# Layer 0 of a two-layer attention kernel: products in 128x32 column tiles, scores in 32x64 tiles

## The chip, the cores and the metric

One core of one Trainium2 chip. The metric is the device time of one execution in microseconds (us), median of three runs.

## The reference, cut to what matters

The input is one block of 128 rows, 256 tokens in a row, 256 channels at a token, in float32. Two layers follow one another; each normalizes over groups of channels, attends within each row, and adds its result to its input.

Layer 0, for every one of the 128 rows (R = 256 tokens, 8 heads of 32 channels):

```
xn = group_norm(x)
gate = sigmoid(xn @ gate_proj); q, k, v = split(xn @ qkv_proj)
sim = softmax(q k^T / sqrt(32)) + bias          # bias: from pair_repr, the same for all rows
out = ((sim v) * gate) @ out_proj
x = x + out
```

Layer 1 does the same without gate and bias, with 4 heads of 64 channels, biases on its projections, and a band: a token sees only tokens up to 16 places away.

## The kernel before, in words

TensorE does all the products; everything is float32. A matrix product in the code becomes two MATMUL and two LDWEIGHTS instructions in the trace (line 784 is passed 2048 times, and the profile has 4096), so every count below is twice that of the code.

In layer 0 a step of the loop over `s` (line 913) takes one row. The engines' order of work is written out by hand: the loop is inside `tc.manual_schedule` (line 903), and each of TensorE, ScalarE and VectorE takes its instructions in the order of the calls. GpSimd and the DMA queue of SyncE are ordered by the framework. TensorE's order in a step is:

1. `scores(s, 0)` (line 777): q and k of four heads. The four heads lie on four strips of 32 partitions, so each product has 32 contraction rows and 128 output columns: a 32x128 tile, and the four heads j use four row strips side by side and write four PSUM banks `sims[j]`. Line 784 does it for two halves `kt` of the keys. ScalarE takes the exponentials from PSUM (line 797).
2. `sum_heads(s - 1)` (line 822): the softmax sums `zs` (line 830) and the product of the bias with v, `bv` (line 816, through `products`), for the row before. These have 128 contraction rows and 32 output columns (one head): 128x32 tiles, four side by side for j = 0 to 3.
3. `attend(s - 1)` (line 853): the product of the exponentials with v, `av`, also through line 816 in 128x32 tiles. VectorE then scales and gates (lines 861, 862, 864) and writes `at`, the input of the output projection.
4. `scores(s, 1)`: the other four heads, again 32x128.
5. `stretch` (line 885): the projections of a coming pair of rows, q and k in even steps, v and gate in odd ones, by `two_of_them` (line 616) with two `Seven` objects. A `Seven` makes a product of two rows by two blocks of channels from seven 128x128 products instead of eight (`product`, line 585). For q, k and the gate (line 594) the weights are the stationary operand and 256 tokens stream; for v (line 598, `by_token`) 128 tokens are the stationary operand and 128 weight columns stream. Between the sevens' last products, `next(po, None)` puts in the output projection of the row before (`one_by_one`, line 702; the product is line 708).

All of step 5 uses the whole array, 128 contraction rows by 128 output columns.

Banks of PSUM: `psum(banks0, "0", 5, 0)` (line 346) gives five banks that score tiles and projections take in rotation, and one each for `zs`, `bv` and `av`. Layer 1 uses the class `Summed`, which inherits `product` from `Seven`, and `one_by_one` for its last rows. Its own products for v (line 1045), scores (1066), attention (1107) and sums (1119) are in tiles of 128x64, 64x64 and 64x32.

Of the kernel before, what the change touches and what calls it, by code (L numbers as in the profile page):

```python
# [15 lines left out]
P = 128  # L16
# [4 lines left out]
H0, D0 = 8, 32  # L21
H1, D1 = 4, 64
BAND = 16
A, B = 4, 32
KB = 64
# [14 lines left out]
def conv_preact_kernel(  # L40
# [14 lines left out]
    nc = tc.nc  # L55
# [20 lines left out]
    def proj_bank(name):  # L76
        return bank("proj", name)

    def sim_bank(name):
        return bank("sim", name)  # L80
# [27 lines left out]
    out_sb = const.tile([P, 2, C], F32, name="out_sb")  # L108
# [29 lines left out]
    for base, per_row, per_group in ((0, 1, -CG), (CG - 1, -1, CG)):  # L138
        nc.gpsimd.affine_select(
            out=within.rearrange("p (g c) -> p g c", c=CG), in_=within.rearrange("p (g c) -> p g c", c=CG),  # L140
# [4 lines left out]
    w_out_t = const.tile([P, 2, C], F32, name="w_out_t")  # L145
# [8 lines left out]
    class Quarters:  # L154


        def __init__(self, pool, source, col, name):
            self.source, self.col = source, col
            self.sums = pool.tile([P, len(NS), P], F32, name=f"sums_{name}")
# [406 lines left out]
    def row_sums(t, x, engine):  # L566
# [3 lines left out]
        engine.tensor_tensor(t[:, 2], x[:, 3], x[:, 2], ALU.subtract)  # L570
        engine.tensor_tensor(t[:, 3], x[:, 1], t[:, 1], ALU.subtract)

    class Seven:


        def __init__(self, pool, weights, x, t, name, tag, by_token=False):
            self.weights, self.x, self.t, self.by_token, self.name = weights, x, t, by_token, name
# [7 lines left out]
        def product(self, n, two=None, first=False):  # L585
            x, t = self.x, self.t
            moving = {1: x[:, 0], 2: x[:, 1], 3: x[:, 3], 4: t[:, 3], 5: t[:, 0], 6: t[:, 1], 7: t[:, 2]}[n]
            out = two if n == 2 else self.ps[:, 1 if n in (3, 5) else 0, :]

            first = first or n == 1  # L590
            flags = dict(stop=n in (2, 3, 4), skip_group_check=True)
            weights = self.weights.stationary(n)
            if not self.by_token:
                nc.tensor.matmul(out, lhsT=weights, rhs=moving, start=first, **flags)  # L594
                return
            for t2 in range(2):
                cols = slice(t2 * P, (t2 + 1) * P)
                nc.tensor.matmul(out[:, cols], lhsT=moving[:, cols], rhs=weights, start=first and t2 == 0, **flags)  # L598

        def take(self, what):  # L600
            if what == "15":
# [44 lines left out]
            p.add_mid()  # L646

    class Summed(Seven):

# [47 lines left out]
            if n in (1, 5):  # L699
                amid(n)  # L700

    def one_by_one(w, at, name, done):

        ps = proj_bank(name)
        done(ps)
        for m in range(2):
            for kt in range(2):
                nc.tensor.matmul(  # L708
                    ps[:, m, :], lhsT=w[:, kt, m * P : (m + 1) * P], rhs=at[:, kt, :],
                    start=(kt == 0), stop=(kt == 1),  # L710
                )
                yield
# [10 lines left out]
    with ExitStack() as both:  # L723
# [20 lines left out]
        with ExitStack() as lay0:  # L744
            row = lay0.enter_context(tc.tile_pool(name="row0", bufs=2))
            att = lay0.enter_context(tc.tile_pool(name="att0", bufs=2))
            st, hd, outs = {}, {}, {}
# [29 lines left out]
            def scores(s, half):  # L777
                i, r = divmod(s, 2)
                q, k = res["q", i], res["k", i]
                sims = [sim_bank(f"sim{s}_{half}_{j}") for j in range(4)]  # L780
                for kt in range(2):
                    for j in range(4):
                        p0 = D0 * j
                        nc.tensor.matmul(  # L784
                            sims[j][:, kt, :],
                            lhsT=k[p0 : p0 + D0, 2 * r + half, kt * P : (kt + 1) * P],
                            rhs=q[p0 : p0 + D0, 2 * r + half, :],
                            start=True, stop=True,
                        )
                ex = att.tile([P, 4, 2, R], F32, tag="ex", name=f"ex{s}_{half}", bufs=4)  # L790
                both = att.tile([P, 4, R], F32, tag="both", name=f"both{s}_{half}")
                hd[s, half] = (ex, both)


                def weigh(js):
                    for j in js:
                        nc.scalar.activation(ex[:, j], sims[j], AF.Exp, scale=1.0 / math.sqrt(D0))  # L797

                weigh(range(3))
                return lambda: weigh((3,))  # L800
# [84 lines left out]
            def stretch(names, i, s, rest=lambda: None):  # L885

                po = iter(())
                if s >= 0:
                    po = one_by_one(out_sb, st[s]["at"], f"po{s}", lambda ps: st[s].update(po=ps))
                if 2 * i >= S:  # L890
                    rest()
                    for _ in po:
                        pass
                    return
                f, g = (
                    Seven(row, quarters[w], xns[i], tss[i], f"{w}{i}", w, by_token=(w == "v")) for w in names
                )
                for w, p in zip(names, (f, g)):
                    res[w, i] = p.to
                two_of_them(row, f, g, f"{names}{i}", po, rest)  # L900


            with tc.manual_schedule(engines={mybir.EngineType.PE, mybir.EngineType.Activation, mybir.EngineType.DVE}):
                for s in range(2):
                    normal(s)
                sum_rows(0)
                stretch("qk", 0, -1)
                for s in range(2, 4):
                    normal(s)
                stretch("vg", 0, -1)  # L910
                sum_rows(1)
                most1 = Most(st1, stats1, 3, 1)
                for s in range(S):
                    scores(s, 0)()
                    zs = sum_heads(s - 1)
                    join_tiles(s, 0, 0)
                    divide(s - 1, zs)
                    if s % 2 == 0:
                        e = res["g", s // 2]
                        nc.scalar.activation(e, e, AF.Exp, scale=-1.0)  # L920
                    z = hd[s - 1, "z"][0] if s > 0 else None
                    rest = ((0, 2), (1, 0), (1, 2))
                    if s < S - 1:
                        attend(s - 1)
                        last_exp = scores(s, 1)
                        if s == 4:
                            for weights in quarters1.values():
                                weights.sum()
                        stretch(("qk", "vg")[s % 2], s // 2 + 1, s - 1, last_exp)
                        for half, j in rest:  # L930
                            join_tiles(s, half, j)
                        least(s - 1, z)
                        if s >= S - 3:
                            most1.join(s - S + 3)
                        normal(s + 4)
                        if s % 2 == 1:
                            sum_rows((s + 3) // 2)
                        finish(s - 1)
                    else:

                        scores(s, 1)()
                        for half, j in rest:
                            join_tiles(s, half, j)
                        least(s - 1, z)
                        attend(s - 1)
                load1(0)
                load1(1)
                warm = proj_bank("warm")

                def keep_on(n):  # L950

                    for _ in range(n):
                        nc.tensor.matmul(warm[:, 0, :], lhsT=ident, rhs=out_sb[:, 0, :], start=True, stop=True)

                divide(S - 1, sum_heads(S - 1))
                last_z = hd[S - 1, "z"][0]
                attend(S - 1)
                for s in (S - 2, S - 1):
                    if s == S - 1:
                        keep_on(4)  # L960
                    for _ in one_by_one(out_sb, st[s]["at"], f"po{s}", lambda ps: st[s].update(po=ps)):
                        pass
                    finish(s)
                mean1, rstd1 = channel_columns(st1, most1, 1, keep_on)
                least(S - 1, last_z)
# [5 lines left out]
        with ExitStack() as lay:  # L971
# [3 lines left out]
            st, hd, outs = {s: {} for s in range(S)}, {}, {}  # L975

            weights = [att.tile([P, 2, 2 * WROW], F32, name=f"1p{i}", bufs=1) for i in range(4)]
# [36 lines left out]
            def project(s):  # L1014

                if s < 0:
                    return iter(())
                return one_by_one(w_out_t, st[s]["at"], f"1po{s}", lambda ps: st[s].update(po=ps))

            ats, ats_t, outputs, last_ots = {}, {}, {}, {}  # L1020

# [221 lines left out]
            with tc.manual_schedule(engines={  # L1243
# [12 lines left out]
                for i in range(last):  # L1256
                    s = 2 * i
# [84 lines left out]
    with tc.If(sure < P):  # L1342
        with ExitStack() as lay:
# [4 lines left out]
            for t in range(2):  # L1348
# [4 lines left out]
                out=bv_row.rearrange("p a b -> p (a b)"), in_=b_in[2 * C : 3 * C].partition_broadcast(P)  # L1353
# [130 lines left out]
            for g in range(S // XG):  # L1484
                x3 = two.tile([P, XG, 2, R], F32, tag="x3", name=f"x3_{g}")
                nc.sync.dma_start(out=x3, in_=rows(x1, g * XG, XG))
                for k in range(0, XG, 2):
                    for half in range(2):
                        nc.vector.bn_stats(
                            out=stats2[:, half, (g * XG + k) // 2, :], in_=x3[:, k : k + 2, half, :]  # L1490
# [32 lines left out]
```

## Time and profile before

| what | value |
|---|---|
| median of three runs | 3169.02 us (3168.06 to 3169.51) |
| profiled execution, span from first to last instruction | 3173.6 us |
| before the first scores of layer 0 | 206 us |
| layer 0, the loop over rows | 206 to about 2079 us |
| layer 1 | about 2089 us to the end |
| mean granted TensorE clock | 0.991 of full speed |

The profile gives one execution. PE is TensorE's matmuls, PEld its weight loads, which overlap with them, DVE is VectorE, ACT ScalarE, POOL GpSimd. A tile is written contraction rows by output columns, 32*128 for instance, and a shape behind it is that of the moving operand. The end of a matmul is modelled, so times below are taken between starts.

### The profile page before, as it was taken

What the parts mean: (1) busy time and instruction counts of PE and PEld (TensorE: products, weight loads), DVE (VectorE), ACT (ScalarE), POOL (GpSimd) and SP (SyncE); (2) the same over time, 40 slices, a digit from 0 to 9 for tenths busy, and PEclk for the clock granted to TensorE, in tenths of its full rate; (3) what the DMA queues carried; (4) which work ended last, traced back from release to release, by engine and by line L of the source; (5) the groups of instructions that cost most, each with busy time, mean ns of one, the idle gap of its engine ahead of it and who ended that gap; (6) DMA issues with size and microseconds to landing.
All of it is one profiled execution on the core that took longest, in us unless ns stands there. A gap on an engine that the chain in (4) does not pass through costs nothing.

```text
span 3173.6 us, 87645 instructions
## 1 busy us (share of the span) xinstructions
PE 3097.4 (98%) x36859; PEld 2384.0 (75%) x36859; DVE 2558.2 (81%) x4140; ACT 1870.3 (59%) x4064; POOL 1613.4 (51%) x1651
## 2 busy tenths in 40 slices
PE   7889999999999999999999999999999999999997
PEld 5567777777777777777777777768888888888886
DVE  4669999999999999999999999956666666666665
ACT  4656666666666666666666666645555555555553
POOL 3034444444444444444444444347777777777774
PEclk8989999999999999999999999999999999999999
DMA  9931111111111111111111111004444444444343
GB/s 379 424 109 42 41 41 34 41 35 39 37 35 41 35 39 37 38 38 35 41 34 37 39 37 39 28 28 102 96 101 101 93 99 102 100 97 101 91 100 69
DMA packets 357105, 242.44 MB, mean 76 GB/s; under 512 B 276072, under 2 KB 342112, under 8 KB 350560
## 3 DMA queue, kind: packets, MB, share of 16 engines
q1 hardware_dynamic: 355808, 234.39, 27.1%
q8 instruction: 292, 4.78, 0.6%
q0 software_dynamic: 752, 2.36, 0.2%
q14 instruction: 109, 0.89, 0.1%
q10 hardware_dynamic: 144, 0.00, 0.0%
HBM read 169.09 MB, written 67.62 MB: 75 GB/s over the span
## 4 chain that ended last, share of the span: by engine, by line
PE 91%; DMA 5%; DVE 2%; ACT 1%; issue 0%; POOL 0%; SPq 0%; DVEq 0%; POOLq 0%; ACTq 0%
PE sim L784 9%; PE p1v L1045 7%; PE po L708 7%; PE av L816 7%; PE bv L816 7%; PE p1q L594 6%; PE pv L598 6%; PE p1o L594 6%; PE pq L594 6%; PE p1k L594 6%; PE pk L594 5%; PE pg L594 5%; DMA pr<-in_L_conv_pair_repr_dram 4%; PE zs L830 4%; PE 1sim L1066 3%; PE 1av L1107 3%
## 5 line engine op out<-in xcount | busy, mean ns | idle before, releaser
L797 ACT ACTIVATE ex<-sim 128x512 f32<-128x512 f32 x1024 | 547.5, 605 | 429.9 <-PE sim L784 429.9
L806 DVE TENSOR_TENSOR both<-ex 128x512 f32<-128x512 f32 x512 | 483.9, 984 | 77.0 <-ACT ex L797 77.0
L846 DVE RECIPROCAL d<-d 128x512 f32<-128x512 f32 x128 | 429.2, 3353 | 4.4
L611 POOL TENSOR_TENSOR v<-v,twovg 128x256 f32<-128x256 f32 x64 | 75.4, 1179 | 548.0 <-ACT twovg L630 548.0
L784 PE MATMUL sim<-q,k 32*128 32x256 f32 x4096 | 295.7, 401 | 1.1 <-ACT ex L797 1.1
L708 PE MATMUL po<-at,out_sb 128*128 128x256 f32 x1024 | 285.0, 382 | 4.0 <-DVE at L864 4.0
L784 PEld LDWEIGHTS sim<-q,k 32*128 32x128 f32 x4096 | 186.7, 184 | 102.4 <-issue 95.0
L816 PE MATMUL bv<-bias_sb,v 128*32 128x256 f32 x4096 | 244.5, 379 | 0.7 <-DVE t L861 0.7
L816 PE MATMUL av<-ex,v 128*32 128x256 f32 x4096 | 244.5, 379 | 0.0
L1045 PEld LDWEIGHTS p1v<-w_in_t,1xn 128*64 128x64 f32 x4096 | 222.3, 137 | 21.5 <-PE p1k L594 20.2
L1045 PE MATMUL p1v<-w_in_t,1xn 128*64 128x128 f32 x4096 | 237.7, 274 | 0.3 <-POOL place L980 0.3
L1076 POOL TENSOR_TENSOR 1p<-1ex,seen 128x768 f32<-128x768 f32 x127 | 230.9, 1818 | 13.4 <-ACT 1ex L1074 13.4
L668 ACT ACTIVATE 1q<-p1q,bqk 128x256 f32<-128x256 f32 x192 | 91.1, 474 | 244.4 <-PE p1q L594 244.4
L708 PEld LDWEIGHTS po<-at,out_sb 128*128 128x128 f32 x1024 | 185.7, 191 | 25.4 <-issue 4.3
L1176 DVE TENSOR_TENSOR 1at<-1av,1near 128x512 f32<-128x512 f32 x128 | 82.6, 686 | 148.6 <-DMA 1near<-rz_far 116.7
L816 PEld LDWEIGHTS bv<-bias_sb,v 128*32 128x32 f32 x4096 | 133.2, 110 | 88.7 <-issue 1.1
L611 POOL TENSOR_TENSOR q<-q,twoqk 128x256 f32<-128x256 f32 x64 | 47.6, 744 | 298.5 <-ACT twoqk L630 298.5
L816 PEld LDWEIGHTS av<-ex,v 128*32 128x32 f32 x4096 | 133.2, 110 | 87.8 <-issue 0.3
L766 DVE TENSOR_SCALAR xn<-xt,mean,rstd 128x256 f32<-128x256 f32 x256 | 179.9, 742 | 0.0
L1083 POOL TENSOR_TENSOR 1zp<-1p 128x512 f32<-128x512 f32 x127 | 162.1, 1276 | 10.0
L568 POOL TENSOR_TENSOR 1ts<-1xn 128x256 f32<-128x256 f32 x64 | 47.0, 734 | 234.3 <-ACT 1xn L1006 234.3
L1052 ACT COPY 1v<-p1v 128x512 f32<-128x512 f32 x128 | 75.1, 587 | 135.1 <-PE p1v L1045 131.6
(300 smaller groups left out, 7872.4 us busy)
## 6 DMA issues: line engine op xcount, KB each, us to landing
pr<-in_L_conv_pair_repr_dram SPq DMA_DIRECT2D x32, 1024.0 KB
xs<-in_x_dram SPq DMA_DIRECT2D x16, 2048.0 KB
x<-o SPq DMA_DIRECT2D x64, 512.0 KB
yg<-x SPq DMA_DIRECT2D x64, 512.0 KB
out_dram<-1o SPq DMA_DIRECT2D x256, 128.0 KB
xg<-in_x_dram SPq DMA_DIRECT2D x252, 128.0 KB
1near<-rz_far SPq DMA_DIRECT2D x124, 256.0 KB
rz_far<-1rz SPq DMA_DIRECT2D x124, 4.0 KB
```

The lines of the kernel that those rows point to most:

```text
L594: nc.tensor.matmul(out, lhsT=weights, rhs=moving, start=first, **flags)
L598: nc.tensor.matmul(out[:, cols], lhsT=moving[:, cols], rhs=weights, start=first and t2 == 0, **flags)
L708: nc.tensor.matmul(ps[:, m, :], lhsT=w[:, kt, m * P : (m + 1) * P], rhs=at[:, kt, :], start=(kt == 0), stop=(kt == 1),)
L766: nc.vector.tensor_scalar(xns[i][:, 2 * r + half, :], xt[:, half, :], mean0[:, half : half + 1], rstd0[:, half : half + 1], op0=ALU.subtra ...
L784: nc.tensor.matmul(sims[j][:, kt, :], lhsT=k[p0 : p0 + D0, 2 * r + half, kt * P : (kt + 1) * P], rhs=q[p0 : p0 + D0, 2 * r + half, :], sta ...
L797: nc.scalar.activation(ex[:, j], sims[j], AF.Exp, scale=1.0 / math.sqrt(D0))
L806: nc.vector.tensor_tensor(both[:, j : j + 2], ex[:, j : j + 2, 0, :], ex[:, j : j + 2, 1, :], ALU.add)
L816: nc.tensor.matmul(to[D0 * j : D0 * (j + 1), half, :], lhsT=v[:, 2 * r + half, c0 : c0 + D0], rhs=weights(4 * half + j, kt), start=(kt == ...
L846: nc.vector.reciprocal(d, d)
L1045: nc.tensor.matmul(ps[KB * half : KB * (half + 1), b, :], lhsT=xns[i][:, 2 * r + kt, KB * b : KB * (b + 1)], rhs=w_in_t[:, kt, 2 * C + P * ...
L1076: engine.tensor_tensor(p.rearrange("p j (r c) -> p (j r) c", c=WROW)[:, :, 0 : 2 * WSTEP] .rearrange("p r (t c) -> p r t c", c=WSTEP)[:, : ...
L1083: engine.tensor_tensor(zp, p[:, :, 0:R], p[:, :, R : 2 * R], ALU.add)
```

## The change

A helper `in_columns` cuts one product into products of `width` output columns: each takes a slice of the stationary operand's columns, streams the same moving operand, and writes its own strip of PSUM partitions. `Seven.product` and layer 0's `one_by_one` use it with width B = 32, so each 128x128 product becomes four of 128x32. `Summed` and layer 1's `one_by_one` use it with width P = 128, so that there the same single product is issued as before. In `scores`, each 32x128 product becomes two of 32x64 (KB = 64), in the order kt, then c, then j. What is computed, the order of the work and the other engines' instructions stay as they are.

```diff
+    def in_columns(out, lhsT, rhs, width, **flags):
+
+        for c0 in range(0, P, width):
+            cols = slice(c0, c0 + width)
+            nc.tensor.matmul(out[cols], lhsT=lhsT[:, cols], rhs=rhs, **flags)
+
     class Seven:
 
+        WIDTH = B
...
             if not self.by_token:
-                nc.tensor.matmul(out, lhsT=weights, rhs=moving, start=first, **flags)
+                in_columns(out, weights, moving, self.WIDTH, start=first, **flags)
                 return
             for t2 in range(2):
                 cols = slice(t2 * P, (t2 + 1) * P)
-                nc.tensor.matmul(out[:, cols], lhsT=moving[:, cols], rhs=weights, start=first and t2 == 0, **flags)
+                in_columns(out[:, cols], moving[:, cols], weights, self.WIDTH, start=first and t2 == 0, **flags)
...
     class Summed(Seven):
 
+        WIDTH = P
...
-    def one_by_one(w, at, name, done):
+    def one_by_one(w, at, name, done, width):
...
-                nc.tensor.matmul(
-                    ps[:, m, :], lhsT=w[:, kt, m * P : (m + 1) * P], rhs=at[:, kt, :],
+                in_columns(
+                    ps[:, m, :], w[:, kt, m * P : (m + 1) * P], at[:, kt, :], width,
                     start=(kt == 0), stop=(kt == 1),
                 )
...
                 for kt in range(2):
-                    for j in range(4):
-                        p0 = D0 * j
-                        nc.tensor.matmul(
-                            sims[j][:, kt, :],
-                            lhsT=k[p0 : p0 + D0, 2 * r + half, kt * P : (kt + 1) * P],
-                            rhs=q[p0 : p0 + D0, 2 * r + half, :],
-                            start=True, stop=True,
-                        )
+                    for c in range(2):
+                        for j in range(4):
+                            p0, k0 = D0 * j, kt * P + KB * c
+                            nc.tensor.matmul(
+                                sims[j][KB * c : KB * (c + 1), kt, :],
+                                lhsT=k[p0 : p0 + D0, 2 * r + half, k0 : k0 + KB],
+                                rhs=q[p0 : p0 + D0, 2 * r + half, :],
+                                start=True, stop=True,
+                            )
```

The calls of `one_by_one` pass B in layer 0 and P in layer 1.

More of the change, by code (lines that the diff above doesn't have):

```diff
@@ L888, in stretch @@
                 if s >= 0:
-                    po = one_by_one(out_sb, st[s]["at"], f"po{s}", lambda ps: st[s].update(po=ps))
+                    po = one_by_one(out_sb, st[s]["at"], f"po{s}", lambda ps: st[s].update(po=ps), B)
                 if 2 * i >= S:
@@ L960, in conv_preact_kernel @@
                         keep_on(4)
-                    for _ in one_by_one(out_sb, st[s]["at"], f"po{s}", lambda ps: st[s].update(po=ps)):
+                    for _ in one_by_one(out_sb, st[s]["at"], f"po{s}", lambda ps: st[s].update(po=ps), B):
                         pass
@@ L1017, in project @@
                     return iter(())
-                return one_by_one(w_out_t, st[s]["at"], f"1po{s}", lambda ps: st[s].update(po=ps))
+                return one_by_one(w_out_t, st[s]["at"], f"1po{s}", lambda ps: st[s].update(po=ps), P)
             ats, ats_t, outputs, last_ots = {}, {}, {}, {}
```

## The prediction, made before the run

> **What bounds the kernel now.** First the page's busy shares, then the busy time by stage (columns: window, length, busy us and instructions of each engine, granted clock, DMA share, GB/s).
>
> ```profile
> PE 3097.4 (98%) x36859; PEld 2384.0 (75%) x36859; DVE 2558.2 (81%) x4140; ACT 1870.3 (59%) x4064; POOL 1613.4 (51%) x1651
> ```
>
> ```profile
> 210.00:2050.00 1840.00, 1839.97 (x19441) 1373.90 (x19437) 1711.61 (x2000) 1176.15 (x2452) 815.64 (x755) 1.00 0.15 38
> ```
>
> In layer 0 TensorE has a matmul in flight for 1839.97 of 1840 us, at full clock; the chain that ended last is 91% PE. So the time of layer 0 is the sum of TensorE's intervals from start to start. What matters is which of these are longer than the array needs. VectorE is next, with 1711.6 of 1840 (93%). Third, the timeline of TensorE alone over one step (start, length, line, tile, count):
>
> ```profile
> 1009.32 1.03 PE L708 MATMUL po<-at,out_sb 128*128 128x256 f32 x4
> 1010.28 1.15 PE L784 MATMUL sim<-q,k 32*128 32x256 f32 x16
> 1011.35 1.07 PE L830 MATMUL zs<-both,ones 128*32 128x256 f32 x16
> 1012.24 1.91 PE L816 MATMUL bv<-bias_sb,v 128*32 128x256 f32 x32
> 1013.97 1.91 PE L816 MATMUL av<-ex,v 128*32 128x256 f32 x32
> 1015.81 1.15 PE L784 MATMUL sim<-q,k 32*128 32x256 f32 x16
> 1016.88 0.71 PE L598 MATMUL pv<-qkv_sb,xn 128*128 128x128 f32 x4
> 1017.43 0.61 PE L598 MATMUL pv<-sums_v,ts 128*128 128x128 f32 x4
> 1017.88 0.60 PE L594 MATMUL pg<-xn,gate_sb 128*128 128x256 f32 x2
> ```
>
> bv has 32 matmuls in 1013.97 - 1012.24 = 1.73 us: 8 groups of four tiles, 216 ns each. A full 128x128 product of 256 columns is also 216 ns (single starts 1009.321, 1009.537, 1009.753). **So column tiles are no faster in the steady stream**: four of them take the time of one full product. Time is lost only around a change of tile shape: sim has 4 groups (0.86 us) and takes 1011.35 - 1010.28 = 1.07.
>
> Layer 1 shows the same for tiles of other shapes, and one odd gap inside 1av:
>
> ```profile
> 2505.41 0.59 PE L594 MATMUL p1o<-1at,sums_1o 128*128 128x256 f32 x2
> 2505.94 3.71 PE L1045 MATMUL p1v<-w_in_t,1xn 128*64 128x128 f32 x64
> 2509.58 1.56 PE L1066 MATMUL 1sim<-1q,1k 64*64 64x96 f32 x61
> ...
> 2511.02 0.39 PE L1107 MATMUL 1av<-1p,1v 64*64 64x80 f32 x9
> 2511.64 1.30 PE L1107 MATMUL 1av<-1p,1v 64*64 64x96 f32 x54 [0.22 <-issue]
> 2512.87 0.66 PE L1119 MATMUL 1zs<-1zp,place 64*32 64x256 f32 x16
> 2513.46 0.70 PE L594 MATMUL p1q<-1xn,w_in_t 128*128 128x256 f32 x2
> ```
>
> [...] at every change of shape the next weight load starts 303 to 309 ns after the last 256-column matmul, elsewhere weights load ahead. [...] after a change the first matmul waits for its own weights, and its second group comes later than usual by 24 ns (zs, 32 columns: 240 instead of 216), 51 (p1v, 64 columns: 160 instead of 109), 104 (sim and pq, 128 columns: 320 instead of 216). [...] Here it is 6.7 ns (1010.278, .284, .291, .298)[...].
>
> **The change part by part**, in ns, each priced from the spacing of single starts beyond the undisturbed one. A step has two visits to the scores, V1 after the projections and V2 after av.
>
> *Before.* V1: the way in from po 309 - 216 = 93; sim's first load 104; the way out 324 - 216 = 108 (from the start of sim's last group to zs); zs's first load 24. Sum 329. V2: in from av 329 - 216 = 113 (20 more, because the last of four tiles starts 20 after the first); first load 104; out 108; first load of a 128-column projection 104. Sum 429.
>
> *After.* The number of changes of shape is the same: the projections now match zs, bv and av, but the scores stand between them each time. **No drain is removed.** (i) In: 113 for both, as po has four tiles now; V1 loses 20. (ii) Sim's first load, 64 columns: 51, a gain of 53 for each visit. (iii) Out: eight tiles at 6.7 ns spread a group over 47 instead of 20 ns, so the drain begins 27 later: 135. Layer 1's 1zs, in eight tiles of 64x32, shows this spread (2513.109 to .155) and 351 from its last group to the next shape. (iv) First load after the scores, 32 columns: 24 in both; V2 gains 80. Each visit: 113 + 51 + 135 + 24 = 323. A step: 758 - 646 = 112 saved. Of these 126 steps run in the steady stream: **14.1 us**.
>
> (v) The v products (line 598, 128 moving columns) start 111.5 ns apart, a little over the load of 128 columns; p1v, with smaller loads and the same moving size, has 109. I take 109 for 128x32: 1792 matmuls x 2.5 = **4.4 us**. [...] The 256-column products gain nothing: they are at 216.
>
> (vi) More instructions: 5504 projection matmuls become four each and 4096 score matmuls two each: 16512 + 4096 = 20608 more matmuls, as many more loads. A step has 316 pairs (22016 + 8192 + 10240 over 128) in about 14.5 us, 46 ns a pair; the densest stretches are v and the scores, 27 ns a pair. Layer 1 runs 1sim and 1av with four pairs in 82.5 ns, 21 a pair, for 2.7 us at a time in nearly every round, so I cost this at nothing. [...]
>
> (vii) 32x64 is not in this trace. Two tiles share a row strip; if their weights load one after the other, the first group's second half is another 53 - 27 = 26 ns late and the way out too: 256 x 26 = 6.7 us lost. If on the contrary the eight tiles' spread cost nothing, 256 x 27 = 6.9 us would be gained. 1sim in 64x64, also two tiles to a strip, starts its four tiles 7 ns apart and loses only 51 at first: I take the loads as parallel.
>
> Total: 14.1 + 4.4 = 18.5 us. **What is late next:** nothing that I find. VectorE works 13.6 us of each step of 14.62, which becomes 14.47 (94%). Its last product for TensorE, `at`, ends at 1006.17 and po's weights load at 1006.95; the cover shrinks by V2's 0.1 us to about 0.67. The banks: the second stream's first product takes the bank of sims[0], freed by ScalarE at 1002.92, and starts at 1003.28; 0.36 becomes about 0.28. The scores' third bank is freed at 1010.11 for a start at 1010.29; both ends move by the same 20 ns. If one were missed, it would cost tens of ns in a step, 126 x 0.03 = 4 us.
>
> The profiled execution's span (3173.6 us; the page gives no time outside it) is 0.14% above the median, 3169.02. The sum is in us of that span, and I take it off the median: 3169.0 - 18.5 = **3150.5 us**.
>
> **Rivals.** First, *half of it*: the weights of two tiles in a strip load in turn (-6.7) and v stays at its loads' pace (-4.4): 18.5 - 11.1 = 7.4 saved, 3161.6 us. For it: no 32x64 here. Against: 1sim and p1v. Second, *slower*: TensorE runs out of instructions. Blocks of instructions come by DMA: one instruction queue of the page has 292 packets and 4.78 MB, 16 KB each. Over the 73718 matmuls and loads that is 65 bytes each, so I take it as TensorE's, some 252 instructions in a block. A step then needs 632 / 252 = 2.5 blocks, some 315 in layer 0, one in 5.8 us. If each left TensorE idle as in the gap inside 1av above, 0.22 us put to issue, that is 69 us: 3150.5 + 69 = 3220 us. It decides from 18.5 / 0.22 = 84 such stalls. For it: that gap. Against: it is the only one of 0.22 so labelled in 1av in 61 rounds, blocks take 1.1 us (median of their packets), and layer 1 draws two within 4 us. Third, *nothing*: VectorE sets the pace at 93% busy, and the gain becomes waits: 3169. Against: its slack above.
>
> **How the numbers follow.** Forecast 0.70, half 0.14, slower 0.11, nothing 0.05. Two runs of this kernel tell 0.2% (6.3 us) apart: faster is below 3162.7. Forecast and half lie below it: 0.84; same 0.05; slower 0.11. The range: the forecast's upper side is 6.9 (spread) lower, 3143.5, and its lower side is the first rival, 3161.6; with both inside, 0.16 is left out. 3143 to 3162.
>
> **What would show it.** PE matmuls 36859 + 20608 = 57467. Two steps take 29.252 us from scores to scores now (14.573 + 14.679); 28.96 after. Sim to zs 1.05 instead of 1.07, sim to pv 1.05, then the first v group 0.13 instead of 0.21; v groups 109 ns apart. Wrong would be: a second group of sim at 290 or more after the first, v groups at 112 or more, "issue" before matmuls inside a stream, or PE waiting for DVE at po.

## The result, and the profile after

The changed kernel takes 3152.52 us (median of four, 3150.13 to 3153.9) against 3169.27 us: 16.75 us less, a ratio of 0.9943 with a 95% interval of 0.9929 to 0.9957. Measured again beside the first experiments below, it took 3152.26 us against 3172.3, a ratio of 0.9937 (0.9923 to 0.9950). The forecast was 3150.5 us.

The page's head for the changed kernel:

```profile
span 3152.1 us, 128861 instructions
...
PE 3075.5 (98%) x57467; PEld 2114.1 (67%) x57467; DVE 2544.5 (81%) x4140; ACT 1870.0 (59%) x4064; POOL 1622.5 (51%) x1651
...
q8 instruction: 453, 7.42, 1.0%
```

57467 matmuls are exactly the count worked out, and the instruction queue went from 292 to 453 blocks. The busy time by stage in layer 0 of the changed kernel (columns as before):

```profile
210.00:2030.00 1820.00, 1819.94 (x39727) 1111.77 (x39720) 1699.80 (x2004) 1177.69 (x2455) 825.68 (x755) 1.00 0.15 39
```

TensorE still has a matmul in flight for all but 0.06 us of this and VectorE is still below it, 1699.8 of 1820 (93%). In layer 0's loop TensorE was recorded as waiting for VectorE's `at` only twice, for 4.1 us in all, and before the change also twice, for 4.0 us, both times in the last steps. So the bound has not moved, and the intervals between starts tell where the time went. TensorE's timeline of one step after:

```profile
1013.01 1.05 PE L577 MATMUL po<-at,out_sb 128*32 128x256 f32 x16
1013.99 1.12 PE L794 MATMUL sim<-q,k 32*64 32x256 f32 x32
1015.04 1.07 PE L840 MATMUL zs<-both,ones 128*32 128x256 f32 x16
1015.93 1.91 PE L826 MATMUL bv<-bias_sb,v 128*32 128x256 f32 x32
1017.65 1.91 PE L826 MATMUL av<-ex,v 128*32 128x256 f32 x32
1019.49 1.12 PE L794 MATMUL sim<-q,k 32*64 32x256 f32 x32
```

And the second visit of an odd step, where v's products follow:

```profile
1005.00 1.12 PE L794 MATMUL sim<-q,k 32*64 32x256 f32 x32
1006.05 0.65 PE L577 MATMUL pv<-qkv_sb,xn 128*32 128x128 f32 x16
1006.51 0.62 PE L577 MATMUL pv<-sums_v,ts 128*32 128x128 f32 x16
1006.95 0.61 PE L577 MATMUL pg<-xn,gate_sb 128*32 128x256 f32 x8
```

bv still takes 1.72 us: four column tiles cost what they cost before. A visit to the scores takes 1.05 us where it took 1.07; the first four v groups 0.46 where the first four v products took 0.55. All that was gained stands at these seams and in v's pace.

One line of the waits can mislead. After the change they put 25.9 us of idle time before the scores' weight loads down to VectorE; before the change nearly all of this idle time, 95.0 us, was "issue":

```profile
PEld sim L794 <- issue: 79.3, 193, 0.8
...
PEld sim L794 <- DVE d L855: 25.9, 63, 0.4
```

The line of before:

```profile
PEld sim L784 <- issue: 95.0, 255, 0.6
```

From the last av matmul to the first score matmul it is 309 or 310 ns in every step of the steady part, with either label, as before the change. So VectorE costs nothing there: the interval is that of the change of shape.

The two profiled executions differ by 21.5 us (3173.6 and 3152.1), more than the medians. Two steps of layer 0 went from 29.252 to 28.955 us, 0.297 less, and 63 such pairs make 18.7 us. 2.8 us more fell in the first step, where the profile of before happened to have a granted clock of 0.76 and that of after 1.00 (time by stage from 206 us). That belongs to this one profile and not to the change: the scores-only kernel, with its projections as before, had 1.00 there too. Layer 1, from its first v product to the start of its last matmul, takes 1074.9 us and 1075.6 us.

### The profile page after: what moved, and what is told of

Same layout as the page of the kernel before. It is cut to its first block, busy times and chain, and to the rows that moved or that the text cites. A ratio compares the mean times of both kernels' runs of the same rounds, so it can differ in the third digit from the quotient of the medians.

```text
span 3152.1 us, 128861 instructions
## 1 busy us (share of the span) xinstructions
PE 3075.5 (98%) x57467; PEld 2114.1 (67%) x57467; DVE 2544.5 (81%) x4140; ACT 1870.0 (59%) x4064; POOL 1622.5 (51%) x1651
## 4 chain that ended last, share of the span: by engine, by line
PE 91%; DMA 5%; DVE 2%; ACT 1%; issue 0%; POOL 0%; SPq 0%; DVEq 0%; POOLq 0%; ACTq 0%
PE sim L794 8%; PE po L577 7%; PE p1v L1055 7%; PE bv L826 7%; PE av L826 7%; PE p1q L577 6%; PE p1o L577 6%; PE pv L577 6%; PE pq L577 6%; PE p1k L577 6%; PE pk L577 5%; PE pg L577 5%; DMA pr<-in_L_conv_pair_repr_dram 4%; PE zs L840 4%; PE 1sim L1076 3%; PE 1av L1117 3%
## 5 line engine op out<-in xcount | busy, mean ns | idle before, releaser
L577 PE MATMUL po<-at,out_sb 128*32 128x256 f32 x4096 | 291.5, 380 | 4.1 <-DVE at L874 4.1
L794 PE MATMUL sim<-q,k 32*64 32x256 f32 x8192 | 288.4, 387 | 1.2 <-ACT ex L807 1.2
L794 PEld LDWEIGHTS sim<-q,k 32*64 32x64 f32 x8192 | 152.1, 131 | 126.9 <-issue 79.3
L1055 PEld LDWEIGHTS p1v<-w_in_t,1xn 128*64 128x64 f32 x4096 | 222.3, 137 | 21.5 <-PE p1k L577 20.2
L577 PEld LDWEIGHTS po<-at,out_sb 128*32 128x32 f32 x4096 | 131.0, 110 | 70.9 <-issue 4.5
L775 DVE TENSOR_SCALAR xn<-xt,mean,rstd 128x256 f32<-128x256 f32 x256 | 160.4, 666 | 0.0
```

The costliest lines, as they stand in the source:

```text
L577: nc.tensor.matmul(out[cols], lhsT=lhsT[:, cols], rhs=rhs, **flags)
L775: nc.vector.tensor_scalar(xns[i][:, 2 * r + half, :], xt[:, half, :], mean0[:, half : half + 1], rstd0[:, half : half + 1], op0=ALU.subtra ...
L794: nc.tensor.matmul(sims[j][KB * c : KB * (c + 1), kt, :], lhsT=k[p0 : p0 + D0, 2 * r + half, k0 : k0 + KB], rhs=q[p0 : p0 + D0, 2 * r + ha ...
L1055: nc.tensor.matmul(ps[KB * half : KB * (half + 1), b, :], lhsT=xns[i][:, 2 * r + kt, KB * b : KB * (b + 1)], rhs=w_in_t[:, kt, 2 * C + P * ...
```

## The experiments

The theory is the prediction's: a change of tile shape costs what I call a drain (about 90 ns by which the first tile of the new shape starts later than the next group of the old one would have) and the first group's own weight load; besides these only the spread of the last group over its tiles (6.7 ns from one to the next) and the pace of v depend on the shape. In both kernels' steady part it is 309 ns from the last tile into the scores and 304 out of them (a ns more in some steps), 93 and 88 over the 216 of a group. The loads show in the trace too: after a change a tile's second load starts 108 ns after its first with 128 columns (the scores before), 55 with 64 (the scores after) and 28 with 32 (zs). The rivals are that drains were saved, that column tiles are faster, and that the supply of instructions takes something back. The period of a step repeats to 1 ns in the traces: of the changed kernel's 124 steps before the last, 60 have exactly 14.460 us and 61 exactly 14.495, the other three 1 ns less. So I compare periods of two steps as well as times.

**The changed kernel again**, no edit.

> The changed kernel once more, as the reference for the runs beside it. Theory (the change gains only at changes of tile shape and in the v products): 3152 us, two steps of layer 0 in 28.955 us. No theory expects anything else.

3152.26 us (five runs), two steps in 28.955 us. It serves as the reference of three runs on the same chip: scores only, projections only, and layer 1's projections in 128x64. The kernel before took 3172.3 us there.

**Scores only.** The diff's part in `scores` put alone into the kernel before:

```diff
-                    for j in range(4):
-                        p0 = D0 * j
...
+                    for c in range(2):
+                        for j in range(4):
+                            p0, k0 = D0 * j, kt * P + KB * c
```

> Only the scores are changed to 32x64; all projections stay 128x128. Theory: each visit gains 53 (first load of 64 instead of 128 columns) and loses 27 (eight tiles spread the last group), so 52 ns in a step and 6.6 us in all: about 3162.6 us, two steps in 29.251 - 0.104 = 29.147 us, V2's first projection still late by 104. Rival (the gain comes from projections that no longer differ in shape from the attention products, so that drains go): no gain here, 3169 us.

3164.62 us, 0.9975 (0.9968 to 0.9983) of the kernel before; two steps in 29.145 us, where the theory had 29.147. V2's first projection still begins with 104 ns too many. The rival that the whole gain comes from matching shapes is out: more than a third of it, 0.107 of 0.297 us in two steps, comes from the scores with no shape matched to another.

**Projections only.** The changed kernel with the scores as before:

```diff
-                    for c in range(2):
-                        for j in range(4):
-                            p0, k0 = D0 * j, kt * P + KB * c
...
+                    for j in range(4):
+                        p0 = D0 * j
```

> Only the projections are changed to 128x32; the scores stay 32x128. Theory: V1 loses 20 (four tiles of po before the drain), V2 gains 80 (first load of 32 instead of 128 columns), two steps gain 120 and the v products another 70 ns: two steps in 29.251 - 0.190 = 29.06 us, in all 12 us: 3157 us. Rival (a change of shape costs less between tiles of 32 columns): the way from po into the scores falls below 309 ns. Rival (column tiles themselves run faster): groups of 256 columns below 216 ns.

3158.17 us, 0.9957 (0.9944 to 0.9971); two steps in 29.062 us, as worked out. From po's last matmul into the scores it is 309 ns in 128x32 as it was in 128x128, so this change of shape drains no faster between narrower tiles. Groups of 256 columns still start 216 ns apart, so column tiles do not run faster either. The gains of the two parts, 0.107 and 0.190 us, add up to the 0.297 of the whole.

**v alone back in 128x128**, so that shapes alternate inside the projections of odd steps:

```diff
-                in_columns(out[:, cols], moving[:, cols], weights, self.WIDTH, start=first and t2 == 0, **flags)
+                in_columns(out[:, cols], moving[:, cols], weights, P, start=first and t2 == 0, **flags)
```

> The changed kernel with v's projection alone back in 128x128, so that v's and the gate's products, which alternate, change the tile shape inside the projections: five times from v to gate or output projection and four times back in an odd step. Theory (every change of shape drains, then waits for its own weights): v to gate 91 + 24, back 113 + 104, the first v load 80 more, v's own pace 70: 5 x 115 + 4 x 217 + 150 = 1.59 us in each of 63 odd steps, 100 us: 3253 us. Rival (a change of the column width alone, with 128 rows in both, needs no drain, only the first loads): 5 x 24 + 4 x 104 + 150 = 0.69 us, 43 us: 3196 us. Rival (shape does not matter): 3157 us.

3253.04 us, 1.0257 (1.0241 to 1.0272) of the kernel before. Even steps are unchanged at 14.460 us, odd ones went from 14.495 to 16.090: 1.595 us more for nine more changes of shape, the larger first load and v's pace; 1.59 was worked out. Without a drain 0.69 was expected. So a change between 128x128 and 128x32, where only the column width differs, drains like the others: from the gate's last matmul to v's first it is 309 ns, as from po to the scores. The scores to v, and v to the gate, in this kernel:

```profile
1016.37 1.12 PE L794 MATMUL sim<-q,k 32*64 32x256 f32 x32
1017.41 0.71 PE L577 MATMUL pv<-qkv_sb,xn 128*128 128x128 f32 x4
1017.96 0.61 PE L577 MATMUL pv<-sums_v,ts 128*128 128x128 f32 x4
1018.50 0.64 PE L577 MATMUL pg<-xn,gate_sb 128*32 128x256 f32 x8
```

The second four v matmuls take 0.54 us to the gate's first, not the 0.45 that they took when the gate had their shape.

**Scores in sixteen tiles of 32x32**, to test the price of the tiles' spread:

```diff
-                    for c in range(2):
+                    for c in range(4):
                         for j in range(4):
-                            p0, k0 = D0 * j, kt * P + KB * c
+                            p0, k0 = D0 * j, kt * P + B * c
```

with `B` for `KB` in the slices.

> The changed kernel with the scores in sixteen tiles of 32x32. Theory (the drain begins when the last tile of the last group ends, and tiles start 6.7 ns apart): the first load falls from 51 to 24, the way out rises from 135 to 189, 27 ns more for each visit, 6.8 us in all: 3159.3 us, two steps in 28.955 + 0.108 = 29.06 us. Rival (the spread of the tiles costs nothing, only loads count): 27 ns less for each visit: 3145.7 us, two steps in 28.85 us. Rival (TensorE's instructions are short): the group spacing rises above 216 ns, and the time well above 3165 us.

3245.73 us, 1.0231 (1.0217 to 1.0245): far from the theory and its first rival, and two steps took 30.455 us. The theory missed a cost of about 350 ns in each visit. Its timeline:

```profile
1009.17 1.49 PE L794 MATMUL sim<-q,k 32*32 32x256 f32 x64
1010.60 1.07 PE L840 MATMUL zs<-both,ones 128*32 128x256 f32 x16
```

A visit takes 1.43 us where it took 1.05. Single starts show how. Fourteen tiles start 6.7 ns apart and the last two 16 apart; the sixteen second matmuls follow in the next group. Then the first tile starts its third matmul at 1009.629, and the second tile only at 1009.822, 193 ns later, its weight load only just before, at 1009.818; the others follow 16.6 ns apart. The second rival, short of instructions, had forecast a time well above 3165 us. But this hole comes in step with the visits, for which a late block of instructions gives no reason: in 252 of 254 visits it stands at the same place, behind the first tile's third matmul, with 193 or 194 ns. Ahead of it lie the first 64 matmuls and loads of the visit and the few of the first tile that follow. A visit in 32x64 has 32 matmuls and 32 loads, 64 in all, and no such hole (in all but two of the changed kernel's visits the eight tiles of each group start at most 8 ns apart); one in 32x32 has 128. So some 64 of them seem to run side by side without a hole: an estimate from these two counts, with no cause shown for it. Two more runs test it.

**Scores in 32x64, by tile**: in the changed kernel, all products of one tile one after another.

```diff
-                for kt in range(2):
-                    for c in range(2):
-                        for j in range(4):
+                for c in range(2):
+                    for j in range(4):
+                        for kt in range(2):
```

> The changed kernel with the score products (32x64) in another order: all that belong to one tile follow one another (c, j, kt in place of kt, c, j). Theory [...]: a visit has exactly 64 (32 matmuls, 32 loads), so all eight tiles still work side by side: two steps in 28.955 us as before, within 0.05. Rival [...]: the tiles of c = 1 start after those of c = 0 have done most of theirs, about 0.5 us more for each visit: two steps in 31 us.

Two steps in 29.167 us (3166.2 us, 0.9979 with 0.9967 to 0.9991): 53 ns more for each visit. The theory's period is missed, since 0.21 us is more than the 0.05 that it allowed; its claim that all eight tiles run side by side holds, and the rival's 31 us is far off. From its second on, each tile starts a matmul every 216 ns. Starts are then not in the program's order: the eighth tile's first matmul starts 100 ns after the visit's beginning, the first tile's second one, which stands ahead of it in the program, after 267. The 53 ns have another cause: eight matmuls and loads now stand between one tile's first and the next tile's first, not four, and the tiles start 13.3 ns apart instead of 6.7. The last group's first and last tile were 46 ns apart and are 97 apart here. The visit grew by that, to within 2 ns. This shows the price of the spread, which the run in 32x32 was meant to show.

**Scores in 32x32, by tile**: the run in 32x32 with the same order.

> The scores in sixteen tiles of 32x32 as in the run before, in the order by tile. Theory [...]: the first 64 instructions are those of eight tiles alone; the ninth tile enters when the first tile's fourth matmul is done, about 1.07 us after the start, so a visit takes some 2.3 us instead of 1.05: two steps in 28.955 + 4 x 1.23 = 33.9 us, about 3460 us in all. Rival ([...]past the first 56 instructions TensorE gets one only every 4.15 ns, as the 16.6 ns of four in the run before suggest): the last tile starts 0.35 us after the first, 0.27 us more for each visit: two steps in 30.0 us, about 3220 us.

3457.69 us, two steps in 33.775 us, against the 33.9 expected.

```profile
1010.99 2.32 PE L794 MATMUL sim<-q,k 32*32 32x256 f32 x64
1013.24 1.07 PE L840 MATMUL zs<-both,ones 128*32 128x256 f32 x16
```

A visit takes 2.25 us (2.3 expected). Eight tiles start between 1010.987 and 1011.088. The ninth does not wait for all four matmuls of the first tile, as I had written: it starts at 1011.412, 27 ns after the first tile's first matmul ended by the record (where ends are modelled). The tenth starts at 1012.068, 1.08 us after the beginning, and the rest every 33 ns. So the first eight tiles, with 64 matmuls and loads, start within 101 ns, and the tenth only when all four matmuls of the first are through (1.07 us after the beginning was worked out for that). This fits the estimate of 64; why it is so, no run shows. The rival (30.0 us) is out.

**Streams in halves**, to strain the supply of instructions: each product of q, k, gate and output projection in layer 0 cut into two halves of its streamed columns.

```diff
+    def in_halves(out, lhsT, rhs, width, start, **flags):
+
+        for h in range(2):
+            part = slice(h * P, (h + 1) * P)
+            in_columns(out[:, part], lhsT, rhs[:, part], width, start=start and h == 0, **flags)
```

`Seven.product` and `one_by_one` call it in place of `in_columns` where the width is B.

> The changed kernel with each product of q, k, gate and output projection in layer 0 cut once more, into two halves of 128 streamed columns: the same work in 3712 x 4 more matmuls and as many more loads, 432 instead of 316 pairs in a step. Theory (the array hides the instructions): two groups of 109 in place of one of 216, 2.3 ns more for each of 3712, 8.5 us: 3161 us. Rival (the supply of instructions costs 0.2 us for each block of some 252 instructions once it is short): 3.4 blocks in a step, up to 95 us more: about 3250 us, with idle time put to issue in the middle of the projections.

3164.49 us, 0.9974 (0.9964 to 0.9984) of the kernel before. 102 of the 124 steps before the last take 14.550 us (14.549 in three of them), 0.145 us more for two, where two groups of 109 for one of 216 make 0.133. The other 22 are longer, by up to 1.8 us each and 6.4 us in all. The two largest gaps stand in the middle of a stream; the one in a gate product:

```profile
346.79 0.40 PE L577 MATMUL pg<-ts,sums_g 128*32 128x128 f32 x8
348.10 0.42 PE L577 MATMUL pg<-ts,sums_g 128*32 128x128 f32 x8 [0.91 <-issue]
```

It waits for no semaphore that the profile shows. In this kernel a block of instructions starts on its way every 4.06 us (median) and takes 1.10 us; the last one before this gap had started 1.14 us before the last matmul ahead of it. Only twice in layer 0's steady part did two blocks start more than 7 us apart, 7.45 and 7.51, and the two largest gaps follow just these two. In the changed kernel there is a block every 5.80 us, and no two starts of matmuls in layer 0's steady part are more than 310 ns apart. So the rival fits what shows here, at 1.37 times the changed kernel's number of pairs, and costs 6.4 us rather than its 95. The profiled execution was the slowest of nine, 5.3 us above their median, so a usual one may lose less. That these gaps are the supply of instructions is inferred from the label and from the blocks' timing; nothing was varied that would show it alone.

**Layer 1's projections in 128x64**, on top of the changed kernel, to use the mechanism where the change did not:

```diff
     class Summed(Seven):
 
-        WIDTH = P
+        WIDTH = KB
```

> The changed kernel, and besides layer 1's projections (q, k and output) in two tiles of 128x64, the shape of its v products. Theory: from the output projection to the v products the shape no longer changes, so the drain (93) and the first load (51) go; after the sums (64x32) the first load is of 64 instead of 128 columns (53 less): 197 ns in each of about 61 rounds, 12 us: 3140.5 us. Rival (drains are hidden in layer 1 by its waits for GpSimd and VectorE, or the extra instructions cost time): 3152 us or more.

3141.01 us, 0.9907 (0.9892 to 0.9923) of the kernel before and 11.3 us under the changed kernel on the same chip. Here a drain is really gone: the projections now have the shape of the v products behind them.

```profile
2510.47 0.63 PE L577 MATMUL p1o<-1at,sums_1o 128*64 128x256 f32 x4
2510.90 3.69 PE L1055 MATMUL p1v<-w_in_t,1xn 128*64 128x128 f32 x64
2514.52 1.55 PE L1076 MATMUL 1sim<-1q,1k 64*64 64x96 f32 x61
```

From p1o's last product to p1v it is 0.43 us for two matmuls in two tiles, where it was 0.53. The median round went from 16.371 to 16.176 us, 195 ns less; 197 were worked out. This version is faster than both kernels: its four times, up to 3144.0 us, all lie below the changed kernel's five on the same chip, 3149.3 and more.

## Why the prediction was right, point by point

The forecast was 18.5 us less. The period of two steps, forecast at 28.96 us, is 28.955. The measured medians differ by 16.75 us, and the interval of their ratio, 13.6 to 22.5 us, holds the forecast; measured again they differ by 20.0. The medians alone could not tell 18.5 from 15, so what speaks for the sum and its terms is the period and the single starts.

| term, ns | forecast | measured |
|---|---|---|
| way into the scores, from 128x32 | 113 | 114 (330 from the last group's first tile, less 216) |
| first load of the scores, 64 columns | 51 | 51 (267) |
| way out, eight tiles | 135 | 134 (350) |
| first load after, 32 columns | 24 | 24 (zs 240, v 133 for 109) |
| v group of 128 columns | 109 | 109 |
| even step, gain | 112 | 113 |
| odd step, gain | 112 + 70 = 182 | 183 |

(i) to (iv): right, each to 1 ns. The heart of it was to see that no drain is saved. Before and after, a step has four changes of shape, and po to scores and av to scores took 309 ns in both kernels. What shrank is the wait for the first weights: 104 to 51 at both visits and 104 to 24 at V2. What grew is the spread of the last group before a drain: by 27 at each visit, and by 20 at the output projection before V1.

(v) v's pace: right. Groups of 128 streamed columns start 109 ns apart with 32 columns in a load as with 64 (p1v), and 111.5 apart with 128. That loads of 128 columns set that pace was my estimate; what the trace has is a tile's second load 108 ns after its first, with 128 columns.

(vi) Instructions: right for this kernel, where no gap stands inside a stream. Its rival was nearer than the prediction had it. With 1.37 times the pairs, gaps appear that look like it; the chance of 0.11 for it was not idle, but its price for each block was far too high: only 22 of 124 steps grew. The third rival, VectorE setting the pace, is out: both kinds of step shrank by what TensorE's intervals lost, 113 and 183 ns, and nothing came late.

(vii) 32x64: right. The weights of two tiles in one row strip load side by side (their loads start 27 ns apart and last 128); otherwise the second group of the scores would have been late by more than 51, and it is not. The spread is not free either: the run by tile paid 53 ns for 51 ns of it. So of the three values that the prediction gave, the middle one, its forecast, was right and the two bounds were wrong.

What the prediction had not seen did not matter here but lay close by, and that it did not matter is luck: a visit in 32x64 has 64 matmuls and loads and its eight tiles start without a hole, where 128 in a visit left one of 193 ns. Cutting the scores once more costs about 93 us, where the price list of the prediction gives 7.

## What to carry to other kernels

Where TensorE is the bound, read its time between starts and not its busy time, and look at each change of tile shape: in layer 0 each cost a drain of about 90 ns (309 or 304 ns from start to start, less 216), and then a wait that grew with the columns of the first weights (24, 51 or 104 ns). Smaller column tiles shorten only the second; giving neighbouring stages one shape removed both in the run with layer 1 in 128x64 (195 ns less in a round, with a smaller first load elsewhere). More tiles are not better without end: the way out counts from the last tile of the last group (134 ns with eight tiles for 108 with four), and while 64 matmuls and loads in a visit ran without a hole here, 128 left one of 193 ns.

## What the runs showed of the hardware that was not expected

Sixteen tiles with 128 matmuls and loads in a visit leave a hole of 193 ns behind about 64 of them (the run in 32x32), and by tile the tenth tile starts 1.08 us after the beginning, when the four matmuls of the first are through. Eight tiles with 64 leave none. By tile in 32x64, tiles do not wait for one another: eight tiles start their first matmuls within 100 ns, ahead of the first tile's second at 267. After a change of shape a tile with four matmuls and loads starts every 6.7 ns, one with eight every 13.3 ns. Later in the 32x32 visits they come at 16.6 ns for four and 33 for eight, some 4.15 ns each. Why the first ones come faster, no run shows. And the clock granted in one step can differ from run to run: 0.76 in the first step of layer 0 in one profile and 1.00 in another, 2.8 us apart.
